# Attention and mixture of experts on one core: the normalised queries turned together with the attention weights

## The chip, the cores and the metric

The kernel runs on one core of a Trainium2 chip. The metric is device time in microseconds (us) of one launch. A core has five engines with queues of their own: TensorE (PE, with its weight loads shown apart as PEld), VectorE (DVE), ScalarE (ACT), GpSimd (POOL) and SyncE (SP), which here only issues DMAs. All data are float32.

## The reference

A cross attention and a mixture of experts, each added to its input. Cut to what matters:

```python
x = x + xattn(ctx_1024, layernorm(x), fside, fside, ...)   # x: 4 x 1024 tokens x 256
x = x + ffn(layernorm(x), Wr, Wg, Wu, Wd)

def xattn(x, latents, shift, scale, ...):      # x: 77 context rows, latents: the tokens
    xn, ln = layernorm(x, w1, b1), layernorm(latents, w2, b2)
    q = ln @ Wq                                # 16 heads of 64
    k, v = split(xn @ Wkv)
    q = q * (1 + scale) + shift
    attn = softmax(einsum('bihd,bjhd->bhij', q, k) / 8)
    return (einsum('bhij,bjhd->bihd', attn, v)) @ Wout

def ffn(x, Wr, Wg, Wu, Wd):                    # 9 experts, inner width 704
    probs = softmax(x @ Wr)
    the two best experts of each token, their weights scaled to a sum of 1
    return sum over them of weight * ((silu(x @ Wg[e]) * (x @ Wu[e])) @ Wd[e])
```

## The kernel before

**What is folded.** Ahead of the tokens the kernel multiplies the query weights into the keys and the output weights into the values. For each of the 4 batches this leaves `g_sb`, 256 rows (as 2 chunks of 128) by 16 x 77 columns for the scores and 9 more for the router's logits, and `u_sb`, which has a row for each head and context row and 256 + 9 columns (`DE`). The 16 x 77 = 1232 rows of `u_sb` are laid out as `KC` = 10 chunks of 128.

**Sub-tiles.** The 4096 tokens are 32 sub-tiles of 128 (`N_SUB`), four to a group (`NG` = 8 groups, `NS` = 4). For sub-tile i:

- `query(i)` (L247, ScalarE) normalises 128 x 255 of `x` into `z`, whose last column is 1. There are two `z` buffers.
- `query_turn(i)` (L256) turns `z` by two transposes on TensorE into PSUM; ScalarE copies the result to `zT`.
- `scores(i, k)` (L264), k = 0, 1, 2: two products each, with the chunks of `zT` as the stationary operand, into one PSUM bank for each k (462, 462 and 317 columns; the last holds the logits of the query part too). VectorE takes the maximum of each head.
- `exponentials(i, k)` (L282, ScalarE): 16 exponentials in all, with their sums.
- `queries_logits(i)` (L293, ScalarE) writes the query's part of the logits into `lg`.
- `attention_weights(i)` (L304, VectorE): the exponentials divided by their sums go to `an`, 128 x 1280. There is one `an`.
- `weights_turn(i)` (L325): one transposition on VectorE, which works in blocks of 32 x 32, from `an` to `anT`; each chunk's elements are written 10 apart. Then a DMA to DRAM, `a_d` (two of them, in turn).
- `weights_back(i)` (L334): four DMAs bring `a_d` back as `aT`, and put the blocks in their places. `aT` has two buffers. The 10 chunks alternate in memory, so a chunk's 128 columns are 10 elements (40 bytes) apart.
- `values(i)` (L344): 10 products with the chunks of `aT` as the stationary operand and `u_sb` as the moving one, 265 columns.
- `attended(i)` (L353, VectorE): one addition of 256 columns to `x` (L357), one of 9 to `lg` (L358).

**The order** is written out by hand (`manual_schedule`): each engine's queue holds its instructions as the code issues them. The main loop (L1486) overlaps sub-tiles. Pass i issues, in this order: `query(i+1)`; `scores` and `exponentials` of i for the banks 0 and 1, with `attention_weights(i-1)` between them; `weights_turn(i-1)`; bank 2; `query_turn(i+1)`; the exponentials of bank 2; `values(i-3)` (`LAG` = 3); then, by the place in the group, statistics of queries, the load of `x` for the group after next, and routing steps of an earlier group (on VectorE and ScalarE); `weights_back(i-1)`; `attended(i-3)`.

**SyncE's queue** holds the DMAs in that order too, and each waits there for its data: a_d, then in one pass of four the load of `x`, in one the store of `x` to the output (L870), in one the normalised tokens `y_d` (L910), which wait for ScalarE's four activations at L906; then the four `aT`. From pass 27 on the first expert's weights (L1217 to L1227) are put between, some in each pass. GpSimd issues gathers and scatters of its own for the experts' lists.

**After attention**, blocks of tokens of one expert run through `hidden_pair` or `hidden_one`, and `down`; their results are added to the output by indirect DMAs. The last three `values` stand among the products of the first block (`in_first`, L1597).

Of the kernel before, what the change touches and what calls it, by code (L numbers as in the profile page):

```python
# [15 lines left out]
P = 128  # L16
# [5 lines left out]
def kernel(  # L22
# [42 lines left out]
    N2 = NP // 2  # L65
    NA = KC * P
    DE = D + E
    HB = TB // J
# [33 lines left out]
    u_d = dram.tile([P, NP * DE], F32, name="u_d")  # L102
    a_d = [dram.tile([P, NA], F32, name=f"a_d{i}") for i in range(2)]
    list_d = dram.tile([ROWS, 2], I32, name="list_d")
# [99 lines left out]
    xg = {}  # L204
# [39 lines left out]

    zTs, exs, sms, lgs, aTs, nmx, fstats, pscs = {}, {}, {}, {}, {}, {}, {}, {}

    def query(i):  # L247

        g, s = divmod(i, NS)
        o, r, _ = zscale[g]  # L250
        nc.scalar.activation(
            zs[i % 2][:, : D - 1], xg[g][:, s, : D - 1], AF.Identity,
            bias=o[:, s : s + 1], scale=r[:, s : s + 1],
        )

    def query_turn(i):  # L256
# [5 lines left out]
        nc.scalar.copy(zT.rearrange("p c t -> p (c t)"), pz[:, : C * P])  # L262

    def scores(i, k):  # L264

        zT = zTs[i]
        h, n = banks[k]
        if k == 0:
            nmx[i] = stat.tile([P, H], F32, tag="mx", name=f"mx{i}")
        psc = pscs[k] = ps_sc.tile([P, TB], F32, tag=f"sc{k}", name=f"psc{i}_{k}")  # L270
        w = n * J + (E if h + n == H else 0)
        for c in range(C):
            nc.tensor.matmul(  # L273
                psc[:, :w], zT[:, c, :], g_sb[i // NS // GPB][:, c, h * J : h * J + w],
                start=(c == 0), stop=(c == C - 1),
            )
        nc.vector.tensor_reduce(  # L277
            nmx[i][:, h : h + n], psc[:, : n * J].rearrange("p (h j) -> p h j", h=n), AX.X,
            ALU.max, negate=True,
        )  # L280
# [12 lines left out]
    def queries_logits(i):  # L293

        g, s = divmod(i, NS)
        if s == 0:
            lgs[g] = pools["rpool"].tile([P, NS, E], F32, tag="lg", name=f"lg{g}")
        n = banks[-1][1] * J
        nc.scalar.activation(
            lgs[g][:, s, :], pscs[len(banks) - 1][:, n : n + E], AF.Copy,  # L300
            scale=zscale[g][2][:, s : s + 1],
        )

    def attention_weights(i):  # L304
# [10 lines left out]
        nc.vector.tensor_tensor(  # L315
            an[:, H * JA :].rearrange("p (m w n) -> p n m w", w=W, n=N2)[:, :, :, :JR],
            ex[:, :, JA:J].rearrange("p (n m) j -> p n m j", n=N2),
# [7 lines left out]
    def weights_turn(i):  # L325


        turned = pools["qpool"].tile([P, NQ, Q, KC], F32, tag="anT", name=f"anT{i}", bufs=1)
        nc.vector.transpose(  # L329
            turned.rearrange("p q t k -> p q k t"), an_of[0].rearrange("p (k q t) -> p q k t", q=NQ, t=Q)  # L330
        )
        nc.sync.dma_start(out=a_d[i % 2], in_=turned.rearrange("p q t k -> p (q t k)"))

    def weights_back(i):  # L334

        aT = aTs[i] = pools["qpool"].tile([P, NQ, Q * KC], F32, tag="aT", name=f"aT{i}")
        there = a_d[i % 2]
        by_key = there.rearrange("(a i) (q m) -> q i a m", i=Q, q=NQ)
        for q in range(NQ):
            nc.sync.dma_start(out=aT[q * Q : (q + 1) * Q], in_=by_key[q])  # L340

    pos = {}

    def values(i):  # L344
        b = i // NS // GPB
        aT = aTs.pop(i).rearrange("p a (t k) -> p (a t) k", k=KC)
        po = pos[i] = mm_tile(f"po{i}")
        for n in range(KC):
            nc.tensor.matmul(  # L349
                po[:, :DE], aT[:, :, n], u_sb[b][:, n, :], start=(n == 0), stop=(n == KC - 1)  # L350
            )

    def attended(i):  # L353

        g, s = divmod(i, NS)
        po = pos.pop(i)
        nc.vector.tensor_tensor(xg[g][:, s, :], po[:, :D], xg[g][:, s, :], ALU.add)  # L357
        nc.vector.tensor_tensor(lgs[g][:, s, :], po[:, D:DE], lgs[g][:, s, :], ALU.add)  # L358

# [1122 lines left out]

    N_SUB = NG * NS
    LAG = 3
    chosen, early = None, None
    for i in range(N_SUB + 1):  # L1486
# [26 lines left out]
        if now_on:  # L1513
# [173 lines left out]
```

## Time and profile before

| | |
|---|---|
| time, median of 3 runs | 885.0 us (884.68 to 886.63) |
| the profiled execution | 887.22 us |
| its span, first to last instruction | 885.2 us |
| granted clock of TensorE, mean | 0.996 of full speed |
| busy, share of the span | PE 98%, DVE 67%, ACT 40%, POOL 35% |
| DMA | 181.20 MB, 205 GB/s on average |
| scores of sub-tiles 1 to 31 (L273), from the first start | 59.58 to about 342 us |
| transposes of the queries (L260) | 64 records, 272 ns median |
| copies zT (L262, ScalarE) | 32, 397 ns median |
| transposition of the weights (L329, VectorE) | 32, 2490 ns median |

A record's duration on TensorE overlaps the next one's, so what an instruction takes of a pass is read from start to start. The columns of a timeline are: start in us, duration in us (of the run of equal instructions, where several are merged), engine, line, operation, output<-input, shape, count; in brackets the idle time of the engine before it and what ended it. A row of a group gives: line, engine, operation, output<-input, shapes and count, then busy us and mean ns of one, then the idle time before them. A row of waits gives the total, the number and the longest.

### The profile page before, as it was taken

What the parts mean: (1) busy time and instruction counts of PE and PEld (TensorE: products, weight loads), DVE (VectorE), ACT (ScalarE), POOL (GpSimd) and SP (SyncE); (2) the same over time, 40 slices, a digit from 0 to 9 for tenths busy, and PEclk for the clock granted to TensorE, in tenths of its full rate; (3) what the DMA queues carried; (4) which work ended last, traced back from release to release, by engine and by line L of the source; (5) the groups of instructions that cost most, each with busy time, mean ns of one, the idle gap of its engine ahead of it and who ended that gap; (6) DMA issues with size and microseconds to landing.
All of it is one profiled execution on the core that took longest, in us unless ns stands there. A gap on an engine that the chain in (4) does not pass through costs nothing. (4 is left out here: it accounts for less than half of the span.)

```text
span 885.2 us, 13820 instructions
## 1 busy us (share of the span) xinstructions
PE 863.1 (98%) x3864; PEld 676.0 (76%) x3864; DVE 590.8 (67%) x1806; ACT 356.4 (40%) x1500; POOL 313.0 (35%) x325
## 2 busy tenths in 40 slices
PE   7999999999999999999999999999999999999996
PEld 6645787787878778987887777777777777778885
DVE  4857688998989988456445666666666666664641
ACT  3668787978879686241111111111111111111110
POOL 3000000404314350147665435435435444454332
PEclk9999999999999999999999999999999999999999
DMA  6117556667676696978788889769779777779722
GB/s 226 50 56 216 147 169 198 167 210 184 173 203 171 179 243 210 307 239 188 172 241 238 233 260 290 229 213 330 217 223 308 227 224 217 219 230 322 211 24 24
DMA packets 132956, 181.20 MB, mean 205 GB/s; under 512 B 26951, under 2 KB 98127, under 8 KB 132752
## 3 DMA queue, kind: packets, MB, share of 16 engines
q1 hardware_dynamic: 115322, 162.90, 60.2%
q0 software_dynamic: 17344, 17.29, 10.3%
q8 instruction: 31, 0.51, 0.2%
q14 instruction: 45, 0.37, 0.1%
q10 hardware_dynamic: 214, 0.13, 0.0%
HBM read 141.54 MB, written 40.41 MB: 206 GB/s over the span
## 5 line engine op out<-in xcount | busy, mean ns | idle before, releaser
L1291 PE MATMUL pg<-xT,wgu 128*128 128x256 f32 x1144 | 252.7, 379 | 1.6 <-DVEq L1640 1.5
L1291 PEld LDWEIGHTS pg<-xT,wgu 128*128 128x128 f32 x1144 | 215.7, 190 | 31.0 <-issue 1.9
L288 ACT ACTIVATE ex<-psc,mx 128x77 f32<-128x77 f32 x512 | 158.8, 331 | 59.1 <-DVE mx L277 58.9
L1371 PE MATMUL po<-wd,hid 128*128 128x256 f32 (+1 forms) x804 | 180.8, 380 | 0.0
L1371 PEld LDWEIGHTS po<-wd,hid 128*128 128x128 f32 (+1 forms) x804 | 149.2, 187 | 28.0 <-issue 3.7
L990 POOL DMA_INDIRECT list_d<-r_entry,r_pli x64 | 65.8, 1028 | 262.6 <-DVE r_pli L977 136.5
L349 PE MATMUL po<-u,aT 128*128 128x265 f32 x640 | 155.5, 398 | 1.2 <-DMA aT<-a_d 1.2
L1264 DVE STREAM_TRANSPOSE xT<-yin 32x128 f32<-32x128 f32 (+1 forms) x544 | 148.3, 273 | 11.4 <-DMA yin<-y_d,ids 3.2
L1406 POOL DMA_INDIRECT out_dram<-co,ids x63 | 100.8, 1601 | 152.0 <-DVE co L1374 127.9
L349 PEld LDWEIGHTS po<-u,aT 128*128 128x128 f32 x640 | 148.6, 312 | 1.4 <-issue 1.4
L273 PE MATMUL psc<-g,zT 128*128 128x462 f32 (+1 forms) x384 | 140.9, 513 | 1.6 <-ACT zT L262 1.5
L1297 ACT ACTIVATE sl<-pg 128x256 f32<-128x256 f32 x130 | 49.8, 384 | 226.6 <-PE pg L1291 203.0
L1298 DVE TENSOR_TENSOR hid<-pg,sl 128x256 f32<-128x256 f32 x130 | 55.0, 424 | 126.2 <-ACT sl L1297 125.5
L273 PEld LDWEIGHTS psc<-g,zT 128*128 128x128 f32 x384 | 72.1, 190 | 59.0 <-issue 45.8
L288 ACT ACTIVATION_READ_ACCUMULATOR ex<-psc,mx 128x1 f32 x512 | 108.2, 211 | 0.0
L329 DVE STREAM_TRANSPOSE anT<-an 128x1280 f32<-128x1280 f32 x32 | 79.6, 2487 | 2.4 <-DMA a_d<-anT 2.3
L1234 POOL DMA_INDIRECT yin<-y_d,ids x67 | 71.0, 1060 | 24.7 <-issue 18.9
L277 DVE TENSOR_REDUCE mx<-psc 128x6 f32<-128x462 f32 (+1 forms) x96 | 53.4, 556 | 23.2 <-PE psc L273 23.2
L1374 DVE TENSOR_SCALAR co<-po,ids 128x256 f32<-128x256 f32 x67 | 32.2, 483 | 52.6 <-PE po L1371 51.0
L310 DVE TENSOR_TENSOR an<-ex,rs 128x1024 f32<-128x1024 f32 x32 | 39.2, 1225 | 1.1
L1359 ACT COPY hid<-ph 128x384 f32<-128x384 f32 x15 | 7.2, 479 | 78.4 <-PE ph L1354 78.4
L1335 ACT ACTIVATE hs<-psg 128x512 f32<-128x512 f32 x15 | 9.0, 597 | 65.3 <-PE psg L1331 65.3
(311 smaller groups left out, 762.8 us busy)
## 6 DMA issues: line engine op xcount, KB each, us to landing
wgu<-in_L_ffn_Wg_dram SPq DMA_DIRECT2D x41, 704.0 KB
wd<-in_L_ffn_Wd_dram SPq DMA_DIRECT2D x41, 640.0 KB
wgu<-in_L_ffn_Wu_dram SPq DMA_DIRECT2D x41, 512.0 KB
a_d<-anT SPq DMA_DIRECT2D x32, 640.0 KB
aT<-a_d SPq DMA_DIRECT2D x128, 160.0 KB
wgu<-in_L_ffn_Wu_dram SPq DMA_DIRECT2D x41, 128.0 KB
x<-in_x_dram SPq DMA_DIRECT2D x8, 512.0 KB
out_dram<-x SPq DMA_DIRECT2D x8, 512.0 KB
```

The lines of the kernel that those rows point to most:

```text
L273: nc.tensor.matmul(psc[:, :w], zT[:, c, :], g_sb[i // NS // GPB][:, c, h * J : h * J + w], start=(c == 0), stop=(c == C - 1),)
L277: nc.vector.tensor_reduce(nmx[i][:, h : h + n], psc[:, : n * J].rearrange("p (h j) -> p h j", h=n), AX.X, ALU.max, negate=True,)
L288: nc.scalar.activation(exs[i][:, h + q, :], pscs[k][:, q * J : (q + 1) * J], AF.Exp, bias=nmx[i][:, h + q : h + q + 1], accum_out=sms[i][: ...
L329: nc.vector.transpose(turned.rearrange("p q t k -> p q k t"), an_of[0].rearrange("p (k q t) -> p q k t", q=NQ, t=Q))
L349: nc.tensor.matmul(po[:, :DE], aT[:, :, n], u_sb[b][:, n, :], start=(n == 0), stop=(n == KC - 1))
L990: i = nc.gpsimd.indirect_dma_start(out=list_d[:, :], out_offset=bass.IndirectOffsetOnAxis(ap=place_i[:, s : s + 1], axis=0), in_=entry.bit ...
L1234: return nc.gpsimd.indirect_dma_start(out=dst, out_offset=None, in_=src, in_offset=bass.IndirectOffsetOnAxis(ap=offsets, axis=0), **kw,)
L1264: yield nc.vector.transpose(xT[q : q + Q].rearrange("p c (h t) -> p h c t", t=P)[:, :nh, :, a : a + Q], of(yins, j)[a : a + Q].rearrange(" ...
L1291: nc.tensor.matmul(pg[:, g, :], w[:, c, at : at + P], xT[:, c, :], start=(c == 0), stop=(c == C - 1),)
L1298: made = nc.vector.tensor_tensor(hid[:, f, :], pg[:, 1, :], sl, ALU.mult)
L1371: nc.tensor.matmul(po[rows, :D], hid[:, f, at], d[:, f, :], start=(f == 0), stop=(f == NF))
L1406: i = nc.gpsimd.indirect_dma_start(out=out_r, out_offset=bass.IndirectOffsetOnAxis(ap=rows_of(j, h, rows), axis=0), in_=cos[j][:, h, :], i ...
```

## The change

The two chunks of the normalised query become chunks 10 and 11 of `an`, which has `KT` = 12 chunks. From sub-tile 4 on (`RIDE` = `LAG` + 1) `query(i)` writes there. In pass i it is now called for sub-tile i+2, so that the queries of i+2 and the weights of i-1 are turned by one transposition, written to `a_d` and read back together as `aT`, with a chunk's columns 12 elements (48 bytes) apart. `scores(i)` takes its stationary operand from the last two chunks of `aT` of sub-tile i-3. `values` of these takes the first ten. Sub-tiles 0 to 3 still go through `query_turn`; the weights of sub-tiles 0, 29, 30 and 31 have no queries beside them and move as 10 chunks.

The logits `lg` become columns 256 to 264 of the tile of `x`, which holds 265 columns for a token. `attended` is then one addition of 265 columns. `x` is loaded and stored as rows of 256 out of 265.

```diff
+    KT = KC + C
+    N_SUB = NG * NS
+    LAG = 3
+    RIDE = LAG + 1
...
-    a_d = [dram.tile([P, NA], F32, name=f"a_d{i}") for i in range(2)]
+    a_d = [dram.tile([P, KT * P], F32, name=f"a_d{i}") for i in range(2)]
...
-        an_of.append(q.tile([P, NA], F32, name="an", bufs=1))
-        for z in zs:
+        an_of.append(q.tile([P, KT * P], F32, name="an", bufs=1))
+        for an in an_of:
+            nc.gpsimd.memset(an[:, H * JA : NA], 0.0)
+        for z in zs + [an[:, NA:] for an in an_of]:
             nc.gpsimd.memset(z[:, D - 1 : D], 1.0)
-        for an in an_of:
-            nc.gpsimd.memset(an[:, H * JA :], 0.0)
...
     def load_x(g):
-        xg[g] = pools["xpool"].tile([P, NS, D], F32, tag="x", name=f"x{g}")
+        both = pools["xpool"].tile([P, NS, DE], F32, tag="x", name=f"x{g}")
+        xl[g], xg[g], lgs[g] = both, both[:, :, :D], both[:, :, D:]
         nc.sync.dma_start(out=xg[g], in_=x_v[g])
...
     def query(i):
         g, s = divmod(i, NS)
         o, r, _ = zscale[g]
+        z = zs[i % 2] if i < RIDE else an_of[0][:, NA:]
         nc.scalar.activation(
-            zs[i % 2][:, : D - 1], xg[g][:, s, : D - 1], AF.Identity,
+            z[:, : D - 1], xg[g][:, s, : D - 1], AF.Identity,
             bias=o[:, s : s + 1], scale=r[:, s : s + 1],
         )
...
+    def turned_query(i):
+        if i < RIDE:
+            return [zTs[i][:, c, :] for c in range(C)]
+        aT = with_queries(aTs[i - LAG], KT)
+        return [aT[:, :, KC + c] for c in range(C)]
...
     def scores(i, k):
-        zT = zTs[i]
+        zT = turned_query(i)
...
-                psc[:, :w], zT[:, c, :], g_sb[i // NS // GPB][:, c, h * J : h * J + w],
+                psc[:, :w], zT[c], g_sb[i // NS // GPB][:, c, h * J : h * J + w],
...
     def weights_turn(i):
-        turned = pools["qpool"].tile([P, NQ, Q, KC], F32, tag="anT", name=f"anT{i}", bufs=1)
+        n = chunks_of(i)
+        turned = pools["qpool"].tile([P, KT * P], F32, tag="anT", name=f"anT{i}", bufs=1)[:, : n * P]
         nc.vector.transpose(
-            turned.rearrange("p q t k -> p q k t"), an_of[0].rearrange("p (k q t) -> p q k t", q=NQ, t=Q)
-        )
-        nc.sync.dma_start(out=a_d[i % 2], in_=turned.rearrange("p q t k -> p (q t k)"))
+            turned.rearrange("p (q t k) -> p q k t", q=NQ, t=Q),
+            an_of[0][:, : n * P].rearrange("p (k q t) -> p q k t", q=NQ, t=Q),
+        )
+        nc.sync.dma_start(out=a_d[i % 2][:, : n * P], in_=turned)
+
+    def chunks_of(i):
+        return KT if RIDE <= i + LAG < N_SUB else KC
 
     def weights_back(i):
-        aT = aTs[i] = pools["qpool"].tile([P, NQ, Q * KC], F32, tag="aT", name=f"aT{i}")
-        there = a_d[i % 2]
+        n = chunks_of(i)
+        aT = aTs[i] = pools["qpool"].tile([P, KT * P], F32, tag="aT", name=f"aT{i}")
+        there = a_d[i % 2][:, : n * P]
         by_key = there.rearrange("(a i) (q m) -> q i a m", i=Q, q=NQ)
         for q in range(NQ):
-            nc.sync.dma_start(out=aT[q * Q : (q + 1) * Q], in_=by_key[q])
+            nc.sync.dma_start(
+                out=aT[q * Q : (q + 1) * Q, : n * P].rearrange("p (a m) -> p a m", a=NQ),
+                in_=by_key[q],
+            )
+
+    def with_queries(aT, n):
+        return aT[:, : n * P].rearrange("p (s k) -> p s k", k=n)
...
     def values(i):
         b = i // NS // GPB
-        aT = aTs.pop(i).rearrange("p a (t k) -> p (a t) k", k=KC)
+        aT = with_queries(aTs.pop(i), chunks_of(i))
...
-        nc.vector.tensor_tensor(xg[g][:, s, :], po[:, :D], xg[g][:, s, :], ALU.add)
-        nc.vector.tensor_tensor(lgs[g][:, s, :], po[:, D:DE], lgs[g][:, s, :], ALU.add)
+        nc.vector.tensor_tensor(xl[g][:, s, :], po[:, :DE], xl[g][:, s, :], ALU.add)
...
         if now_on:
-            if 0 < i < N_SUB - 1:
+            if 0 < i < RIDE - 1:
                 query(i + 1)
+            if 1 < i < N_SUB - 2:
+                query(i + 2)
...
-            if 0 < i < N_SUB - 1:
+            if 0 < i < RIDE - 1:
                 query_turn(i + 1)
```

More of the change, by code (lines that the diff above doesn't have):

```diff
@@ L197, in open_attention @@
         zs.extend(q.tile([P, D], F32, name=f"z{i}", bufs=1) for i in range(2))
-        an_of.append(q.tile([P, NA], F32, name="an", bufs=1))
-        for z in zs:
+        an_of.append(q.tile([P, KT * P], F32, name="an", bufs=1))
+        for an in an_of:
+            nc.gpsimd.memset(an[:, H * JA : NA], 0.0)
+        for z in zs + [an[:, NA:] for an in an_of]:
             nc.gpsimd.memset(z[:, D - 1 : D], 1.0)
-        for an in an_of:
-            nc.gpsimd.memset(an[:, H * JA :], 0.0)
-    xg = {}
+    xg, xl, lgs = {}, {}, {}
     def load_x(g):
-        xg[g] = pools["xpool"].tile([P, NS, D], F32, tag="x", name=f"x{g}")
+        both = pools["xpool"].tile([P, NS, DE], F32, tag="x", name=f"x{g}")
+        xl[g], xg[g], lgs[g] = both, both[:, :, :D], both[:, :, D:]
         nc.sync.dma_start(out=xg[g], in_=x_v[g])
@@ L243, in query_scale @@
         zscale[g] = (off_mean("qo", g, mv, r), r, sd)
-    zTs, exs, sms, lgs, aTs, nmx, fstats, pscs = {}, {}, {}, {}, {}, {}, {}, {}
+    zTs, exs, sms, aTs, nmx, fstats, pscs = {}, {}, {}, {}, {}, {}, {}
     def query(i):
@@ L295, in queries_logits @@
         g, s = divmod(i, NS)
-        if s == 0:
-            lgs[g] = pools["rpool"].tile([P, NS, E], F32, tag="lg", name=f"lg{g}")
         n = banks[-1][1] * J
@@ L315, in attention_weights @@
         nc.vector.tensor_tensor(
-            an[:, H * JA :].rearrange("p (m w n) -> p n m w", w=W, n=N2)[:, :, :, :JR],
+            an[:, H * JA : NA].rearrange("p (m w n) -> p n m w", w=W, n=N2)[:, :, :, :JR],
             ex[:, :, JA:J].rearrange("p (n m) j -> p n m j", n=N2),
@@ L1481, in listed @@
         yield from places(g)
-    N_SUB = NG * NS
-    LAG = 3
     chosen, early = None, None
```

## The prediction

> S(n) is the start of the scores of sub-tile n on TensorE; pass n is from S(n) to S(n+1). In it TensorE also does values(n-3), and VectorE turns the weights of sub-tile n-1. KB is 1,000 bytes.
>
> **What bounds the kernel now.** I read the busy table by stage first: from 130 to 300 us TensorE is busy 169.86 of 170 us at a granted clock of 1.00, VectorE 154.77, ScalarE 135.59, and the DMA engines have a share of 0.67. So inside attention TensorE sets the pace. Then the timeline of TensorE, an ordinary pass and the end of the stage:
>
> ```profile
> 207.72 4.33 PE L273 MATMUL psc<-g,zT 128*128 128x462 f32 x12
> 211.88 0.38 PE L260 MATMUL pz<-ident,z 128*128 128x128 f32 x2
> 212.10 4.84 PE L349 MATMUL po<-u,aT 128*128 128x265 f32 x20
> 216.78 4.33 PE L273 MATMUL psc<-g,zT 128*128 128x462 f32 x12
> ...
> 318.52 4.33 PE L273 MATMUL psc<-g,zT 128*128 128x462 f32 x12
> ...
> 327.60 4.33 PE L273 MATMUL psc<-g,zT 128*128 128x462 f32 x12
> 331.77 0.38 PE L260 MATMUL pz<-ident,z 128*128 128x128 f32 x2
> 333.33 4.93 PE L349 MATMUL po<-u,aT 128*128 128x265 f32 x20 [1.18 <-DMA aT<-a_d]
> ```
>
> Start to start, a pass is 9.06 us: scores 4.16, query transposes 0.22 (the printed 0.38 overlaps), values 4.68. No gap, but one: S(30) is 327.60, and values(27) waited 1.18 us for its weights to come back from DRAM. Hence the queue of the DMAs next, where the first column is the issue:
>
> ```profile
> 242.57 0.34 SPq L332 DMA_DIRECT2D a_d<-anT  x1
> 246.60 0.34 SPq L910 DMA_DIRECT2D y_d<-y  x1
> 247.61 2.52 SPq L340 DMA_DIRECT2D aT<-a_d  x4
> ...
> 316.55 0.34 SPq L332 DMA_DIRECT2D a_d<-anT  x1
> 320.91 0.34 SPq L910 DMA_DIRECT2D y_d<-y  x1
> 321.45 0.39 SPq L1219 DMA_DIRECT2D wgu<-in_L_ffn_Wu_dram  x1
> ...
> 323.29 1.92 SPq L340 DMA_DIRECT2D aT<-a_d  x4
> ```
>
> The way back (aT) stands in line behind y_d, which waits for ScalarE, and at the end behind the first experts' weights as well. Last, VectorE's waits between 160 and 308 us, its whole slack in 16 passes:
>
> ```profile
> DVE mx L277 <- PE psc L273: 6.0, 6, 1.1
> DVE x L357 <- PE po L349: 1.1, 3, 0.4
> ```
>
> **The change, part by part.**
>
> *Removed from TensorE:* the two transposes of sub-tiles 4 to 31, 28 x 0.22 = 6.2 us, all on the path; 25 of them (5.5 us) stand ahead of S(28). The Trainium skill ("VectorE: DVE Perf Modes", "Rules for kernel authors") speaks against the change: a 128x128 transpose belongs on TensorE where PSUM will do. Its section "The three transpose paths" has 390 ns there; that would give 28 x 2 x 0.39 = 21.8 us. The row says 0.11 us each beside other matmuls, so 6.2; I take the row, which makes the removed work cheap and the rule right here.
>
> *ScalarE* loses the copy zT (0.40 us in each of 28 passes) and still writes z, now into an. It has 20% idle time; worth nothing directly.
>
> *VectorE:* the transpose of 10 chunks takes 2.34 us to the next start (203.37 to 205.69, 221.66 to 224.01); 12 chunks 2.81, so +0.47. The two additions take 0.33 + 0.08 to the next start; one over 265 columns 0.34, so -0.07. Net +0.40, or 6.4 us in 16 passes, where the slack is 7.1 and TensorE would need 16 x 0.22 = 3.5 less. 7.1 - 3.5 - 6.4 = -2.8: VectorE alone would hold back 2.8 of those 3.5 us. Behind it stand the exponentials, and the turned weights themselves.
>
> *The round trip.* Bytes rise from 655 to 786 KB each way. Without other traffic a_d takes 3.0 us from its issue to that of aT (187.49 to 190.49), and aT's data in quarter-microsecond windows end 4.0 us after its first issue. They flow at some 215 GB/s in 512 packets, a_d's at about 430: a fifth more bytes in as many packets is between +0.3 (half of the packet's time is fixed) and +0.6 us; I take 0.4. What matters is the deadline: aT(n-3) was needed at values, 4.4 us into pass n; now scores(n) itself waits for it, and two passes before it are 0.22 shorter. All of TensorE's queue stands behind that wait: scores, values(n-3), then the reductions and exponentials.
>
> In the passes with y_d (8, 12, 16, 20, 24) the data of aT end at about 141.8, 180.1, 216.2, 252.7 and 289.8 by the same windows; 0.5 us for the receipt is an estimate from a_d, whose data end that long before the next issue. Against S(10), S(14), S(18), S(22), S(26) of 143.40, 180.09, 216.78, 253.46 and 290.38 the slack is 1.1, -0.5, 0.1, 0.2, 0.1. Take off 0.4 for the later y_d (it follows VectorE's lengthened row), 0.4 for the bytes, 0.44 for the shorter passes: waits of 0.1, 1.7, 1.1, 1.0, 1.1, together 5.0 us. VectorE's 2.8 lie within these, since it catches up while TensorE waits. The other passes keep 1.6 us or more, or come just behind such a wait.
>
> *The end.* aT(27) came at 333.2, S(28) + 23.8 (S(28) = 309.38). Its y_d is held by ScalarE there, which loses a copy, so only the bytes count: +24.4 for S(30), which was S(28) + 18.2. From there scores and values take 8.9, so S(31) is at +33.3 instead of +28.7: **4.6 us lost**, the old wait of 1.18 already taken out. aT(28) is issued at 334.81 and its data end near 339.8, S(28) + 30.4, in time. TensorE then runs without a gap to 406 us, and its later waits (1.77 us for yin at 414.85) are for gathers that follow the same work; nothing absorbs the delay.
>
> *Strides.* The scores' weights were contiguous and now step 48 bytes. The page shows what stepping (40 bytes) does to a load:
>
> ```profile
> L349 PEld LDWEIGHTS po<-u,aT 128*128 128x128 f32 x640 | 148.6, 312 | 1.4 <-issue 1.4
> L273 PEld LDWEIGHTS psc<-g,zT 128*128 128x128 f32 x384 | 72.1, 190 | 59.0 <-issue 45.8
> ```
>
> The skill ("SBUF — State Buffer", "Door 1: The DMA port swizzle") explains it by lines of 16 bytes, each crossing paid. By that rule alone 12 loads x 122 ns x 28 = 41 us more; by the timeline loads of 312 ns keep a pitch of 234 ns in values, under the scores' 385 and 264, so nothing shows. I take nothing. That 48 bytes load as 40 do, no row shows: between 0 and, in proportion to the step, 20 x 47 ns x 28 = 26 us. Both cross a line at each element; I take 0. A faster load is bounded too: contiguous ones ran 256 columns in 216 ns, 223 for 265, so at most 20 x 11 ns x 28 = 6 us gained.
>
> *x* lies in rows of 265, so its loads and the stores out of it move 1 KB instead of 4 KB at a time: at aT's rate 524 KB take 2.4 us instead of 1.3. They stand behind a_d in passes with slack. Before S(29) the store may cost a microsecond, inside the wait of S(30), which doesn't hang on S(29). Set-up (one more column of ones) is off the path.
>
> **Sum:** -5.5 + 5.0 + 4.6 = +4.1; I say 4.0. The profiled execution took 887.22 us, 2.0 around its span of 885.2, and lies 2.2 above the median of the runs (885.0); it would become 891.2, the median **889.0**.
>
> **Rivals.**
> - *The loop is in time, the end is not* (the receipt is shorter, VectorE keeps up): -5.5 + 4.6 = -0.9, 884.1. For it: the slack of 0.1 to 1.1 is read from windows. Against: VectorE's waits are nearly used up. 0.17.
> - *Faster, the trip home hidden:* aT(27) gets past the weights in front of it. With landing at S(28) + L the end costs L - 19.7 (24.3 gives 4.6). With the loop in time the change is over 0.2% faster from L under 23.4; wholly in time it is -6.2 - 1.2 = -7.4, 877.6; half-way 881. For it: what is in flight together need not land in order. Against: even the old, later wait was overrun. 0.13.
> - *Slower, the step of 48 bytes:* each 10 ns on the values' pitch of 234 costs 5.6 us: from 895. For it: no row has it. Against: the line rule. 0.15.
> - The forecast, 886 to 892: 0.55.
>
> About 0.2% (1.8 us) can be told from no change. Faster: 0.13 and 0.04 of the first rival, 0.17. Same: its other 0.13 and the low end of the forecast, 0.19. Slower: 0.64. The range, 883.5 to 895, leaves out most of the second rival and the far part of the third.
>
> **What would show it.** TensorE waiting "<-DMA aT" ahead of scores, not values: about 6 us at S(30), about 1 in each y_d pass. Passes without a wait of 8.84 us; transposes of 2.96 us on average record (2.49 now); VectorE's waits shorter. I am wrong if scores never wait for aT, or if the pitch of values leaves 234 ns.

## The result, and the profile after

| | before | after |
|---|---|---|
| median of 4 runs | 885.82 us (884.68 to 889.48) | 914.63 us (910.78 to 918.43) |
| ratio, 95% interval | | 1.0304 (1.0278 to 1.033) |
| profiled execution | 887.22 us | 912.32 us |
| its span | 885.2 us | 910.6 us |
| granted clock of TensorE, mean | 0.996 | 0.994 |
| start to S(4) | 89.0 us | 87.5 us |
| S(4) to S(27) | 210.8 us | 230.1 us |
| S(27) to S(31) | 38.4 us | 44.9 us |
| S(31) to the last instruction | 547.1 us | 548.1 us |

The change costs 3.0%. The loss lies wholly between S(4) and S(31), where the changed path runs: 275.0 us instead of 249.1. Set-up and experts differ by about a microsecond each.

The groups of the page after, in the order line, engine, operation, output<-input, count, then busy us and mean ns of one:

```profile
L371 PEld LDWEIGHTS po<-u,aT 128*128 128x128 f32 x640 | 170.8, 361 | 0.5 <-issue 0.4
...
L285 PEld LDWEIGHTS psc<-g,aT 128*128 128x128 f32 x336 | 109.6, 347 | 23.6 <-issue 10.5
```

A load for `values` took 312 ns on average before and takes 361 now; those for the scores that ride took 190 and take 347. TensorE's timeline after shows what comes of it. The first five lines run from `values` of pass 12 to `values` of pass 14, the last one is S(29):

```profile
168.54 5.48 PE L371 MATMUL po<-u,aT 128*128 128x265 f32 x20
173.86 4.38 PE L285 MATMUL psc<-g,aT 128*128 128x462 f32 x12
178.08 5.48 PE L371 MATMUL po<-u,aT 128*128 128x265 f32 x20
185.46 6.26 PE L285 MATMUL psc<-g,aT 128*128 128x462 f32 x12 [1.90 <-DVE x L379]
191.56 5.48 PE L371 MATMUL po<-u,aT 128*128 128x265 f32 x20
...
340.45 6.05 PE L285 MATMUL psc<-g,aT 128*128 128x462 f32 x12 [2.99 <-DMA aT<-a_d]
```

Start to start, `values` takes 5.32 us (168.54 to 173.86) where it took 4.68, though nothing waits: 266 ns for each of its 20 matmul records (its 10 products are recorded as two each) instead of 234. The scores take 4.21 us, and the query transposes between the two are gone. An ordinary pass is 9.53 us instead of 9.06. Then there is the wait ahead of S(14) at 185.46 and of S(29) at 340.45. The bracket at 185.46 names `x L379`, the addition `attended(10)`, whose result these scores don't use. In the packet records of the DMAs the last packet of the aT that they do use ended at 184.65, 0.81 us before the start; ahead of S(18), S(22), S(26) and S(30) it ended 0.57 to 0.73 us before, whatever the bracket names. So it is aT that came last. The queue of the DMAs after:

```profile
171.95 0.34 SPq L344 DMA_DIRECT2D a_d<-anT  x1
175.82 0.34 SPq L931 DMA_DIRECT2D y_d<-y  x1
178.05 2.27 SPq L356 DMA_DIRECT2D aT<-a_d  x4
```

The read that S(14) needs is issued at 178.05, 6.1 us after its a_d, and the scores start 7.4 us later.

After a long wait the scores themselves are slow. Three windows of 1 us after S(14), not adjoining: columns are the window, then busy us (with the count) of PE, PEld, DVE, ACT and POOL, the granted clock, the DMA share and GB/s.

```profile
187.00:188.00 1.00, 1.00 (x3) 0.59 (x2) 0.00 (x0) 0.00 (x0) 0.00 (x0) 0.50 0.54 186
189.00:190.00 1.00, 1.00 (x2) 0.36 (x1) 1.00 (x2) 1.00 (x9) 0.00 (x0) 0.50 0.71 123
191.00:192.00 1.00, 1.00 (x5) 1.00 (x5) 1.00 (x2) 0.64 (x5) 0.00 (x0) 1.00 0.77 149
```

The granted clock is 0.50 at 187 and 189 us and back at 1.00 at 191. These scores take 6.10 us (185.46 to 191.56), 1.89 more than others. Those of S(29) take 5.89 (340.45 to 346.34).

**VectorE** was to become the tight engine. Its waits between 160 and 308 us after, with total, number and longest:

```profile
DVE mx L289 <- PE psc L285: 13.0, 10, 2.6
DVE x L379 <- PE po L371: 2.4, 5, 0.9
```

Its waits come to 15.4 us instead of 7.1: TensorE became slower by more than VectorE did.

### The profile page after: what moved, and what is told of

It reads as the page before. It is cut to its first block, busy times and chain, and to the rows that moved or that the text cites. A ratio compares the mean times of both kernels' runs of the same rounds, so it can differ in the third digit from the quotient of the medians.

```text
span 910.6 us, 13650 instructions
## 1 busy us (share of the span) xinstructions
PE 881.6 (97%) x3808; PEld 735.6 (81%) x3808; DVE 602.7 (66%) x1774; ACT 349.1 (38%) x1472; POOL 314.6 (35%) x326
## 5 line engine op out<-in xcount | busy, mean ns | idle before, releaser
L371 PE MATMUL po<-u,aT 128*128 128x265 f32 x640 | 174.4, 428 | 0.0
L371 PEld LDWEIGHTS po<-u,aT 128*128 128x128 f32 x640 | 170.8, 361 | 0.5 <-issue 0.4
L1011 POOL DMA_INDIRECT list_d<-r_entry,r_pli x64 | 66.9, 1045 | 279.8 <-DVE x L379 131.7
L285 PE MATMUL psc<-g,aT 128*128 128x462 f32 x336 | 126.9, 528 | 9.0 <-DMA aT<-a_d 4.8
L285 PEld LDWEIGHTS psc<-g,aT 128*128 128x128 f32 x336 | 109.6, 347 | 23.6 <-issue 10.5
L340 DVE STREAM_TRANSPOSE anT<-an 128x1536 f32<-128x1536 f32 (+1 forms) x32 | 91.5, 2858 | 0.1
L289 DVE TENSOR_REDUCE mx<-psc 128x6 f32<-128x462 f32 (+1 forms) x96 | 53.6, 558 | 38.7 <-PE psc L285 38.3
```

Source lines behind the costliest of these rows:

```text
L285: nc.tensor.matmul(psc[:, :w], zT[c], g_sb[i // NS // GPB][:, c, h * J : h * J + w], start=(c == 0), stop=(c == C - 1),)
L289: nc.vector.tensor_reduce(nmx[i][:, h : h + n], psc[:, : n * J].rearrange("p (h j) -> p h j", h=n), AX.X, ALU.max, negate=True,)
L340: nc.vector.transpose(turned.rearrange("p (q t k) -> p q k t", q=NQ, t=Q), an_of[0][:, : n * P].rearrange("p (k q t) -> p q k t", q=NQ, t=Q),)
L371: nc.tensor.matmul(po[:, :DE], aT[:, :, n], u_sb[b][:, n, :], start=(n == 0), stop=(n == KC - 1))
L1011: i = nc.gpsimd.indirect_dma_start(out=list_d[:, :], out_offset=bass.IndirectOffsetOnAxis(ap=place_i[:, s : s + 1], axis=0), in_=entry.bit ...
```

## The experiments

The theory after the result: the step of 48 bytes makes `values` slow, and waits are added. Rivals were that `values` slows because SBUF or the DMA engines carry more in this kernel, and, for the waits, that the order of SyncE's queue makes them, that the extra bytes do, or that something else holds up the DMA engines.

The runs fall into five groups, each on one chip and beside its own runs of the kernel before: 888.68 us in group 1, 886.71 in group 2, then 903.23, 899.82 and 902.89 on other chips. On these the stage after S(31) is longer (562 to 566 us instead of 547). The loop agrees better: before_planes and before_spread, whose orders differ little, take 209.4 and 209.3 us from S(4) to S(27) on two chips. So totals are compared within a group, and stages over all. The medians of after_planes_sel, before_planes, planes_order, after_spread, before_spread, after_best and after_best_gated are of 4 to 10 executions; every other kernel of the groups has one, and so has the kernel before in group 1. Executions of one kernel lie up to 8 us apart (after_planes_sel 891.74 to 899.98), so a total of one execution shows only large differences. Stages are read from one profiled execution each; the starts within a trace show the small differences.

| kernel | total us | S(4) to S(27) | S(27) to S(31) | S(4) to S(31) |
|---|---|---|---|---|
| before | 887.22 | 210.8 | 38.4 | 249.1 |
| after | 912.32 | 230.1 | 44.9 | 275.0 |
| *group 1, before 888.68* p11 | 892.88 | 219.6 | 38.3 | 257.9 |
| p12 | 909.18 | 228.8 | 39.9 | 268.7 |
| p13 | 901.61 | 223.3 | 38.9 | 262.2 |
| e2 | 906.70 | 228.3 | 45.2 | 273.5 |
| *group 2, before 886.71* after_planes | 912.98 | 228.1 | 44.9 | 273.0 |
| after_selected | 898.53 | 219.9 | 41.1 | 261.0 |
| before_planes | 885.17 | 209.4 | 40.5 | 249.9 |
| after_planes_sel | 896.62 | 215.0 | 41.2 | 256.2 |
| *group 3, before 903.23* after_no_scatter | 918.86 | 222.2 | 41.0 | 263.2 |
| noquery | 898.39 | 201.5 | 43.1 | 244.6 |
| noquery_dve | 905.73 | 204.9 | 43.4 | 248.3 |
| planes_order | 904.65 | 213.2 | 36.5 | 249.6 |
| *group 4, before 899.82* after_spread | 926.63 | 226.2 | 44.6 | 270.8 |
| before_spread | 899.73 | 209.3 | 37.0 | 246.3 |
| after_best | 913.47 | 222.8 | 36.4 | 259.2 |
| *group 5, before 902.89* after_gated | 928.52 | 223.0 | 47.1 | 270.1 |
| after_best_gated | 915.12 | 223.4 | 39.9 | 263.3 |

### The step alone: p11, p12, p13

In the kernel before, a chunk's columns become 11, 12 or 13 elements apart; the places between hold zeros, and nothing rides there. The round trip carries the added bytes.

```diff
+    STEP_K = 12
-    a_d = [dram.tile([P, NA], F32, name=f"a_d{i}") for i in range(2)]
+    a_d = [dram.tile([P, STEP_K * P], F32, name=f"a_d{i}") for i in range(2)]
...
-            turned.rearrange("p q t k -> p q k t"), ...
+            turned[:, :, :, :KC].rearrange("p q t k -> p q k t"), ...
...
-        aT = aTs[i] = pools["qpool"].tile([P, NQ, Q * KC], F32, tag="aT", name=f"aT{i}")
+        aT = aTs[i] = pools["qpool"].tile([P, NQ, Q * STEP_K], F32, tag="aT", name=f"aT{i}")
...
-        aT = aTs.pop(i).rearrange("p a (t k) -> p (a t) k", k=KC)
+        aT = aTs.pop(i).rearrange("p a (t k) -> p (a t) k", k=STEP_K)
```

> The kernel before, with the ten chunks of anT, a_d and aT laid 12 elements apart (two empty columns between, 786 KB each way instead of 655); queries still go through TensorE, nothing rides. Theory (the step of 48 bytes makes the loads of the stationary operand slower): the 20 matmuls of values take 5.3 us of a pass as in the kernel after, against 4.68 before, in all 32 sub-tiles; weight loads of L349's group about 370 ns; time about 885 + 32 x 0.64 = 905 us. Rival (the step is harmless; the added bytes or the riding queries did it): values stay at 4.68 us, time within 2 us of before.

> The kernel before with the chunks 11 elements (44 bytes) apart. If a load costs in proportion to the step: values 4.68 x 1.1 = about 5.0 us a pass, time about 894 us. If it hangs on how the step falls on memory banks (a multiple of 16 bytes being bad, an odd step good): values at 4.68 us or less, time as before within 2 us.

> The kernel before with the chunks 13 elements (52 bytes) apart, more bytes than in the kernel after. In proportion to the step: values about 5.8 us a pass, loads about 400 ns, time about 915 us or more. By banks: an odd step is good, values at 4.68 us or less, time 885 to 888 us.

Measured: 909.18, 892.88 and 901.61 us against 888.68. The loads of `values`, shortest, median and longest in ns, in the tile view of `aT`; p12 first, then p11, then p13:

```profile
L352 PEld LDWEIGHTS po<-u,aT x640: 341/369/373, 84.2 to 391.5; 128*128 128x128 f32 x160
```

```profile
L352 PEld LDWEIGHTS po<-u,aT x640: 320/346/353, 81.3 to 375.9; 128*128 128x128 f32 x160
```

```profile
L352 PEld LDWEIGHTS po<-u,aT x640: 329/357/360, 82.2 to 384.6; 128*128 128x128 f32 x160
```

In p12's timeline `values`, with the query transposes ahead of it as before, reads so:

```profile
193.16 5.64 PE L352 MATMUL po<-u,aT 128*128 128x265 f32 x20
198.64 4.33 PE L276 MATMUL psc<-g,zT 128*128 128x462 f32 x12
```

It takes 5.08 us at a step of 11, 5.48 at 12 and 5.24 at 13, where it takes 4.68 at 10. With nothing riding, and with no wait of TensorE between S(4) and S(31), p12 loses 20.5 us, most of what the change loses, and its pitch of 5.48 us and loads of 369 ns meet the forecast. It is the step and not the bytes that go with it: 13 carries more bytes than 12 and is faster. Nor is it odd against even (11 and 13 are both slower than 10), and in proportion to the step 13 would have taken 5.8 us or more. Which law it follows stays open.

### The read ahead of the store of y: e2

`weights_back(i-1)` is issued right after `values`, so SyncE has it ahead of y_d and of the experts' weights. Against the kernel after:

```diff
+        if 1 < i < N_SUB - 1:
+            weights_back(i - 1)
...
-        if 1 < i < N_SUB - 1:
-            weights_back(i - 1)
```

> The kernel after, with the four reads of aT put on SyncE's queue ahead of the load of x, the store of x, y_d and the first expert's weights of the same pass. Theory (about 13 us of the loss are waits of scores for aT, which is issued behind y_d and the weights): the waits ahead of scores fall from about 13 us to under 3, values stay at 5.32 us, time about 915 - 11 = 904 us. Rival (the waits come from VectorE, which turns the weights too late): the waits stay within 3 us of 13, time about 914 us.

Measured 906.70 us. The stage gains only 1.5 us. SyncE's queue in pass 12 of e2:

```profile
170.06 0.34 SPq L344 DMA_DIRECT2D a_d<-anT  x1
175.35 1.73 SPq L356 DMA_DIRECT2D aT<-a_d  x4
177.18 0.38 SPq L931 DMA_DIRECT2D y_d<-y  x1
```

The order is as wanted, and y_d comes last. Still the read starts only 5.3 us after a_d, because a_d itself is not home, and S(14) follows at 183.06, 7.7 us after the read's issue. Start to start, the waits ahead of S(14) and S(18) are 1.6 and 2.0 us, and the one ahead of S(30) is 4.7 (there the read is issued 9.6 us after its a_d, at 341.48 against 331.89). The order of the queue isn't their main cause; the transfers are slow.

### The chunks in two planes: after_planes, before_planes

Two transpositions of half the chunks each, so that a chunk's columns lie 6 (after) or 5 (before) apart, in two planes. The reads move pieces of 768 or 640 bytes. The core of it, in the kernel before:

```diff
-        nc.vector.transpose(
-            turned.rearrange("p q t k -> p q k t"), an_of[0].rearrange("p (k q t) -> p q k t", q=NQ, t=Q)
-        )
+        by_plane = turned.rearrange("p h (q t k) -> p h q k t", q=NQ, t=Q)
+        chunks = an_of[0].rearrange("p (h k q t) -> p h q k t", h=PLANES, q=NQ, t=Q)
+        for h in range(PLANES):
+            nc.vector.transpose(by_plane[:, h], chunks[:, h])
...
-        by_key = there.rearrange("(a i) (q m) -> q i a m", i=Q, q=NQ)
+        by_key = there.rearrange("(b i) (q m) -> q i b m", i=Q, q=NQ)
```

> The kernel after, with the twelve chunks in two planes of six, so that a chunk's columns are 6 elements (24 bytes) apart instead of 12; the reads from DRAM come in pieces of 768 B instead of 1536. Theory (the step alone slows the loads): values at 4.7 us a pass or less, loads of about 250 ns, the 18 us of the stride come back: about 915 - 18 = 897 us, the waits for aT stay or grow a little. Rival (something else of the change slows values, as the larger tile): values stay at 5.3 us, 914 us.

> The kernel before, with its ten chunks in two planes of five: a step of 20 bytes instead of 40, reads in pieces of 640 B. If the loads bound values before too (234 ns against 223 that 265 columns take by the experts' products): values at 4.47 us a pass, 32 x 0.21 = 6.7 us faster, 878 us. If the 265 columns bound it: as before within 1 us, or a little slower by the smaller pieces.

Measured: after_planes 912.98 against 886.71, before_planes 885.17, a ratio of 0.9974 (0.9955 to 0.9994). The loads in after_planes, tile view of `aT`:

```profile
L376 PEld LDWEIGHTS po<-u,aT x640: 294/297/318, 85.4 to 394.3; 128*128 128x128 f32 x160
```

297 ns instead of 370. Its timeline, passes 12 and 13:

```profile
167.08 4.64 PE L376 MATMUL po<-u,aT 128*128 128x265 f32 x20
171.56 4.33 PE L285 MATMUL psc<-g,aT 128*128 128x462 f32 x12
...
184.99 6.21 PE L285 MATMUL psc<-g,aT 128*128 128x462 f32 x12 [4.62 <-DMA aT<-a_d]
```

`values` takes 4.48 us (167.08 to 171.56) instead of 5.32: the stride's cost is gone, and a pass is 8.65 us. Yet the stage takes 273.0 us against 275.0. The waits ahead of scores have grown from 9.0 to 23.6 us, and scores run at a reduced clock after most of the long ones. The total missed the expectation by 16 us; why a faster pass brought nothing is said under "Why the prediction went wrong".

before_planes contains nothing of the change; it lies 0.26% below the kernel before (0.06 to 0.45%). Its `values` are 0.09 us shorter behind the transposes, no more. Without them 20 records take 4.48 us at steps of 5 and of 6 alike, 224 ns each. That is what the 265 columns would take by the experts' products (216 ns for 256, so 223, an estimate), so at these steps the load seems to bind no longer.

### Only where there is time: after_selected, after_planes_sel

Sub-tiles 10, 14, 18, 22, 26, 29 and 30, whose scores waited, go through `query_turn` again; 21 still ride. In the kernel after:

```diff
+    TURNED = (*range(RIDE), 10, 14, 18, 22, 26, 29, 30)
...
-        z = zs[i % 2] if i < RIDE else an_of[0][:, NA:]
+        z = zs[i % 2] if i in TURNED else an_of[0][:, NA:]
...
-        return KT if RIDE <= i + LAG < N_SUB else KC
+        return KT if i + LAG < N_SUB and i + LAG not in TURNED else KC
```

> The kernel after, with the step of 12 as it is, but sub-tiles 10, 14, 18, 22, 26, 29 and 30, whose scores waited or were forecast to wait for aT, go through TensorE's transposes again; the other 21 ride. Theory (the waits come from reads that share the DMA engines with y_d, the list's scatters and the experts' weights): no wait of over 0.5 us ahead of scores is left, no pass runs at half clock, about 13 us come back and 7 x 0.22 = 1.5 are paid; with 7 passes fewer at the step of 12 another 7 x 0.64 = 4.5 come back: 915 - 16 = 899 us. Rival (VectorE is the limit, and waits move elsewhere): waits of together over 6 us stay, 907 us or more.

> The kernel after with both: planes of six, and the seven sub-tiles through TensorE. If the two causes account for the loss: values at 4.5 to 4.7 us, no waits for aT, 21 x 0.22 = 4.6 us of transposes saved against before, and VectorE gives back some: between 876 and 884 us. If something of the change costs beside these: over 888 us.

Measured: 898.53 and 896.62 us against 886.71; the first meets its forecast of 899, the second misses its own. In after_selected one wait of over 0.5 us is left, 2.7 us ahead of S(31), and the stage is 14.0 us shorter than after's. In its timeline steps of 10 and 12 stand side by side, with and without the query transposes:

```profile
139.06 0.38 PE L267 MATMUL pz<-ident,z 128*128 128x128 f32 x2
139.27 5.64 PE L372 MATMUL po<-u,aT 128*128 128x265 f32 x20
144.75 4.33 PE L286 MATMUL psc<-g,zT 128*128 128x462 f32 x12
148.92 4.72 PE L372 MATMUL po<-u,aT 128*128 128x265 f32 x20
153.48 4.38 PE L286 MATMUL psc<-g,aT 128*128 128x462 f32 x12
```

At a step of 12 `values` takes 5.48 us behind the transposes and 5.32 without; at 10 it takes 4.56 without and 4.68 behind them (212.10 to 216.78 in the kernel before). So the transposes were worth 0.33 us a pass, 0.22 of their own and 0.11 in the `values` behind them, and the step costs 0.75 us a pass, like against like.

after_planes_sel has neither the step nor rides at the places with waits, and the stage is still 256.2 us: there are seven waits again, 11 us in all, at other sub-tiles than before. The five long ones (1.1 to 2.9 us) are ahead of S(15), S(19), S(23), S(27) and S(31), each behind a sub-tile that was taken out.

### What slows the transfers: after_no_scatter, after_spread, after_gated

In the group's routing GpSimd sends eight scatters of 128 pieces of 8 bytes to `list_d` (L1011), one after another. In after_no_scatter the first five groups send none:

```diff
-                if g != NG - 3:
+                if g < NG - 3:
+                    pending.pop()
+                elif g != NG - 3:
                     scatter()
```

> The kernel after without the 40 scatters by which GpSimd writes the places of groups 0 to 4 into the experts' lists, which leaves those tokens without their experts' part. Everything on SyncE stays. Theory (these scatters of 128 pieces of 8 B hold up the DMA engines in the passes with y_d, where the write of a_d took 5.3 us instead of 3.3 and the read 7.7 instead of 4.3): the waits ahead of S(14), S(18), S(22) (2.1, 1.9, 1.6 us) and the pass at half clock after S(14) go, those of S(29) and S(30) stay: attention 6 to 8 us shorter. Rival (y_d itself and its wait for ScalarE hold the read up): waits of 1 us or more stay there.

The total, 918.86 against 903.23, says little, since the experts work from other lists. The stage is 263.2 us, 11.8 shorter than after's. TensorE's timeline and SyncE's queue at the place where after waits:

```profile
178.92 5.48 PE L371 MATMUL po<-u,aT 128*128 128x265 f32 x20
184.24 4.38 PE L285 MATMUL psc<-g,aT 128*128 128x462 f32 x12
```

```profile
172.79 0.34 SPq L344 DMA_DIRECT2D a_d<-anT  x1
176.66 0.34 SPq L931 DMA_DIRECT2D y_d<-y  x1
177.10 2.21 SPq L356 DMA_DIRECT2D aT<-a_d  x4
```

No wait, at the same step and the same bytes. From a_d to the read it is 4.3 us instead of 6.1. The waits ahead of S(14), S(18) and S(22) are gone, and at the end 1.5 (S(29)) and 0.4 us (S(30)) are left. So the scatters hold up the transfers. The packet records show where: without scatters each of the 128 packets of this a_d (sub-tile 11) takes 0.24 us and none over 0.26; with them 25 take over 0.5 us, up to 1.98. Whether the small writes themselves do it, or something else that goes with a scatter, is not shown. VectorE's work is the same in both kernels, so it is not VectorE that made these waits. Nor are the long trips of the change's making. From the issue of a_d to the end of aT's last packet sub-tile 11 takes 12.7 us in after and 9.9 without scatters, but 12.8 in the kernel before and 11.6 in p12, where the same trip made nothing wait.

In after_spread `scatter()` is called twice in each pass instead. It did not spread them: nothing held GpSimd, which started all eight between 166.6 and 177.2 us (166.0 to 175.8 in after). So its stage says nothing of spreading. It is 4.2 us shorter than after's all the same, with waits of 1.5, 0.5 and 0.5 us ahead of S(14), S(18) and S(22), which shows how far two traces with nearly the same order can lie apart.

> The kernel after, with the 8 scatters of a group of tokens into the experts' lists issued two in each of four passes instead of eight in a row. Theory (a row of 1,024 pieces of 8 B stands in the DMA engines in front of a_d and aT; two scatters leave the round trip its slack): the waits of scores of 11.8 us in the attention stage fall to under 4; the stride's cost stays, values at 5.32 us. Rival (the pieces cost the same wherever they stand, and every pass now waits a little): waits stay at 8 us or more.

Measured 926.63, a ratio of 1.0306 (1.0241 to 1.0372). In after_gated each pair waits for the first half of that pass's maxima:

```diff
-                if g != NG - 3:
-                    scatter()
...
+            row_made = scores(i, 1)
...
+            for _ in range(2 if i < N_SUB - 1 else 0):
+                scatter(row_made)
```

> The kernel after, with the scatters really two to a pass: each waits for the pass's second row of maxima on VectorE (in after_spread GpSimd had nothing to wait for and still sent all eight within 11 us). If it is eight in a row that hold up the round trip: the waits at the heads of S(14), S(18), S(22) go, the attention stage from S(4) to S(31) takes 264 to 267 us as in after_no_scatter (263.2), against 275.0 in the kernel after. If the number of pieces counts wherever they stand: 270 us or more, with small waits in many passes.

Measured 928.52 against 902.89. GpSimd's timeline now shows pairs, a pass apart:

```profile
172.77 1.11 POOL L1009 DMA_INDIRECT list_d<-r_entry,r_pli  x1 [136.74 <-DVE mx L289]
174.18 1.00 POOL L1009 DMA_INDIRECT list_d<-r_entry,r_pli  x1 [0.30 <-issue]
181.72 0.98 POOL L1009 DMA_INDIRECT list_d<-r_entry,r_pli  x1 [6.55 <-DVE mx L289]
```

No scores up to S(27) wait over 0.3 us, and S(4) to S(27) takes 223.0 us, nearly as without scatters (222.2). So in the loop spreading them is enough. A pair still slows the a_d that it stands beside: 27 of 128 packets of sub-tile 12's take over 0.5 us, and its trip takes 11.0 us instead of 9.9 without scatters; but the passes with y_d no longer carry all eight. The end is worse (47.1 instead of 44.9): the scatters have moved into the last passes, where the waits grew. By this the whole stage, 270.1 us, missed the 264 to 267 of the forecast. It reaches the rival's 270, but without the rival's small waits in many passes.

### What the transposes are worth at most: noquery, noquery_dve

before_planes, in which all sub-tiles from 3 on use the turned query of sub-tile 3: no transposes, no ride, no wait for one.

```diff
-        zT = zTs[i]
+        zT = zTs[min(i, 3)]
...
-            if 0 < i < N_SUB - 1:
+            if 0 < i < 3:
                 query_turn(i + 1)
```

noquery_dve adds on VectorE a transposition of two chunks into a tile that nothing reads.

> The kernel before in two planes of five, with TensorE's query transposes and the copies zT left out from sub-tile 4 on (scores take sub-tile 3's queries), and nothing put on VectorE or the DMAs for them. It shows what TensorE has to gain at most. Theory (transposes cost 0.22 us themselves and 0.11 us in the first loads of values): a pass of 8.65 us, 28 x 0.33 = 9 us less than before_planes, 875 us. Rival (VectorE, 95% occupied, holds already): less than 4 us gained.

> As noquery, and VectorE turns the two chunks of the query as well, into a tile that nobody reads, so that its work is that of the change but no round trip and no stride come with it. Theory (VectorE becomes the limit, as the slack of 0.44 us a pass is used up): the gain of noquery falls by half or more, 880 to 885 us. Rival (VectorE has room): as noquery within 1.5 us.

Measured: S(4) to S(27) 201.5 and 204.9 us, against 209.4 of before_planes. A pass without the transposes is 8.65 us, and the most they can be worth is 7.9 us in these 23 passes. VectorE's two added chunks alone take 3.4 of it back. Over the whole stage 5.3 and 1.6 us are left, since the end waits longer (43.1 and 43.4 us against 40.5); the totals, of one execution each, are 898.39 and 905.73 against 903.23.

### Attempts at a version that beats both: planes_order, before_spread, after_best, after_best_gated

planes_order is before_planes with e2's move; before_spread is before_planes with after_spread's; after_best and after_best_gated are after_planes with after_spread's or after_gated's scatters, and with sub-tiles 29 to 31 through `query_turn`.

> before_planes with the four reads of aT put on SyncE's queue ahead of the load of x, the store, y_d and the experts' weights. Nothing of the change is in it; it is tried as a version that may beat both. If the wait of 1.8 us ahead of values(27) is the queue's: it goes, 883 us against 885. If it is traffic of the DMA engines: no difference.

> before_planes with the scatters spread in the same way, nothing of the change in it. Its round trip has slack almost everywhere, so little is expected: within 2 us of before_planes and before.

> The change with what was found mended: two planes of six, scatters spread, and sub-tiles 29, 30 and 31, which stand behind the experts' weights, through TensorE. If stride and scatters are the whole of the loss: a pass of 8.65 us plus VectorE's share of about 0.1, 25 x 0.3 = 7 us less than before at best. If the pieces of 768 B keep the reads late: waits of scores in several passes, 5 us or more over before.

> after_best with the scatters held back in the same way. If the row of scatters is what the smaller pieces cannot bear: S(4) to S(31) takes 243 to 248 us, less than before's 249, and the time falls 2 to 6 us below before. If the reads of 768 B are late on their own: waits stay, 252 us or more.

Measured ratios to the kernel before: 1.0017 (0.9993 to 1.0041), 0.9997 (0.997 to 1.0024), 1.015 (1.0089 to 1.0212) and 1.0122 (1.0081 to 1.0162). The first two show no difference; the last two remain slower, with stages of 259.2 and 263.3 us instead of the 243 to 248 hoped for. No version with the change came below the kernel before.

## Why the prediction went wrong, by its own steps

The direction was right (slower was the likeliest). The size was not: 28.8 us between the medians, 25.4 between the spans, against 4.0. Stage S(4) to S(31), 27 passes, in the prediction's terms:

| term | forecast us | measured us | from |
|---|---|---|---|
| transposes removed | -5.5 | -8.9 | 27 x 0.33 |
| stride, in `values` | 0 | +20.2 | 27 x 0.75 |
| stride, in scores | 0 | +1.1 | 27 x 0.04 (4.21 against 4.17) |
| waits in the y_d passes | +5.0 | +5.7 | 2.06 + 1.93 + 1.56 + 0.16 |
| slow scores after them | none | +2.5 | 1.89 + 3 x 0.19 |
| end | +4.6 | +4.7 | 3.15 + 1.68 + 1.1 + 0.2, less 1.4 that pass 30 lost before |
| sum | +4.1 | +25.3 | 25.9 measured |

**The step that failed is "Strides", where the sum took 0; the runs show 20.2 us in `values`.** One of the prediction's own signs of being wrong came true: the pitch of `values` left 234 ns, for 266. Its argument was that loads of 312 ns "keep a pitch of 234 ns in values", so that nothing shows, and that 48 bytes load as 40 do. The second half is wrong (369 ns against 312 in p12), and so is the first: it took 312 ns to be harmless, while `values` had no time to spare at it. At steps of 5 and 6 the load is 297 ns and `values` without transposes takes 4.48 us; at 10, 312 ns and 4.57; at 12, 370 ns and 5.32. Something of the load showed at 10 already, and beyond it 58 ns more of load cost 37 ns more of pitch. The Trainium skill's lines of 16 bytes ("SBUF — State Buffer", "Door 1: The DMA port swizzle") would make every step from 16 bytes on alike; here steps of 20, 40, 44, 48 and 52 bytes load in 297, 312, 346, 369 and 357 ns. The measurement decides.

The prediction had written the right bound, 0 to 26 us, and the rival with its price ("each 10 ns on the values' pitch of 234 costs 5.6 us"). 37 ns by that price are 20.7 us, and 20.2 were measured. What went wrong was to take one end of the bound as if a row supported it, and then to end the range at 895, though it was to hold the bounds of what was unknown.

**The transposes** were under-sized, 0.22 us a pass instead of 0.33: the timeline's start to start gives the instruction's own time, and the 0.11 it left in the products behind it can be seen only where both kinds of pass stand in one trace (after_selected). The figure that the prediction weighed ("VectorE: DVE Perf Modes", "The three transpose paths", 390 ns each, given there for bf16) remains far above either, 0.11 or 0.165 us each. VectorE's transposition of 12 chunks takes 2.91 us, close to the 2.96 forecast.

**The waits in the loop** came where they were forecast, at S(14), S(18) and S(22), at almost the sum forecast. That sum is luck, of two misses that offset each other. The prediction read the end of aT's data from windows, where a_d's next data hide the last packets: it took 180.1 and 216.2 us for the passes 12 and 16, while the packet records of the same trace end at 182.00 and 217.88. Read so, S(14) and S(18) would have been given about 3.6 and 2.8 us. Against that the passes were to be 8.84 us and became 9.53, which gave each trip 1.4 us more. The added bytes were under-sized too: an undisturbed trip (sub-tile 13) takes 7.1 us before and 8.1 after, 1.0 more where 0.4 was taken. The cause of the long trips was not named: the prediction saw y_d ahead of the read, and in the same passes the eight scatters were at work, before the change as after it. e2 against after_no_scatter tells the two apart.

**Why a faster pass brought nothing.** The prediction saw that aT falls due earlier, but not what hangs on what: the change closes a ring. `scores(i)` takes its query from `aT(i-3)`, which holds the weights made from `scores(i-3)`. So from S(i-3) to S(i) there must be time for the scores, the exponentials, the weights, the turn and the round trip. Before, the same chain fell due only at `values(i-3)`, 4.4 us into pass i, and so had 3 x 9.06 + 4.4 = 31.6 us; p12 has 34.0 and waits nowhere. Now it has three passes, 28.6 us in after and 26.0 in after_planes (0.6 more where products of the routing fall into them). Where the ring binds, the pace of TensorE drops out. S(14) less S(11) is 31.26 us in after (185.46 - 154.20) and 31.28 in after_planes (184.99 - 153.71); S(18) less S(15) is 31.12 and 31.19; what goes beyond three passes is wait. The smaller pieces of after_planes are not the reason, since its trip takes 12.8 us there, and after's 12.7. Even S(10), with no scatter near, comes 28.02 us after S(7) in after_planes: enough for passes of 9.53 us, too much for 8.65. This accounts for after_planes, and agrees with after_planes_sel, where the waits came back at other sub-tiles. Whether a longer lag, with a third `aT` buffer, would open the ring was not tried.

**The end** cost what was forecast, at S(29) and S(30) instead of S(30) alone, and not mainly for the reason given. With the experts' weights still in the queue, but without the scatters (GpSimd's gathers run earlier there too), 1.9 us of 4.2 are left, and with e2's order, where the read stands ahead of that pass's weights, the wait is 4.7.

**VectorE** did not hold back the changed kernel, since TensorE became slower still. At the pace of the transposes removed it would have: noquery_dve shows 3.4 us in 23 passes, which is 0.15 a pass, near the forecast's 2.8 in 16, though its passes were to shrink by 0.33 us and not by 0.22.

## What to carry to other kernels

A price for which the trace has no row, here a stationary operand at a new step, multiplied by 560 matmul records, is not zero because a rule lets two steps look alike: take the bound into the range, or measure the one load by itself. Before moving data onto a round trip, draw what each start depends on in terms of earlier starts: a ring of three passes makes the trip's time the pace, and speeding up the engine inside it only turns work into wait. And where a transfer is late, look at everything that the DMA engines carry at that time, not only at the queue that it stands in.

## What the runs showed of the hardware

- Median time of one float32 load of 128 x 128 by the step between its columns: contiguous 190 ns, 20 and 24 bytes 297, 40 bytes 312, 44 bytes 346, 48 bytes 369 (343 ahead of the scores' products), 52 bytes 357. The time from one record of `values` to the next, behind query transposes, goes with it: 229 ns at 20 bytes, 234 at 40, 254 at 44, 274 at 48, 262 at 52.
- As work began again after a wait, TensorE's granted clock was in some cases 0.50, for 3.4 us in most of them and 6.8 in a few. By the idle time in brackets ahead of scores, none of those up to 1.77 us was followed by it (S(18) in after). Most of 1.84 us (S(18) in e2) and more were, but not those of 2.21 us (S(27) in planes_order), 2.66 us (S(29) in after_gated) and 2.94 us (S(22) in after_best). So the length of the wait alone does not decide it.
- Eight scatters of 128 pieces of 8 bytes, about 1.3 us apart, carry 8 KB, and beside them the round trip of sub-tile 11 took 12.7 us instead of 9.9. They are on another engine's queue than the transfers they slow. The delay is not a constant: in p12, with as many bytes, the trip took 11.6 us.
